# Rows normed where they are gathered, and a search shared by VectorE and ScalarE over two 15-bit numbers, in a macaron block with two expert layers

## The chip, the cores and the metric

The kernel runs on one core of a Trainium2 chip. Its five engines run side by side, each with its own queue: TensorE (PE; its weight loads are shown as PEld), VectorE (DVE), ScalarE (ACT), GpSimd (POOL) and SyncE (SP), which here only issues DMAs. The metric is the device time of one execution in microseconds, as the median of the runs shown. Everything is float32 unless a type is named.

## The reference

x has 4 x 2048 = 8192 rows of 256. A feed-forward layer of 8 experts, an attention layer, and the same feed-forward layer again are added to it:

```python
x = x + 0.5 * ffn(layernorm(x), router_w, wg, wu, wd)
x = x + attn(layernorm(x), ...)
x = x + 0.5 * ffn(layernorm(x), router_w, wg, wu, wd)
```

The feed-forward layer routes each row to two of eight experts, and each expert takes at most 1280 rows:

```python
probs = softmax(xf @ router_w.T)                  # 8192 x 8
topw, topi = top_k(probs, 2); topw = topw / (topw.sum(-1) + 1e-06)
order = lexsort((-fw, fe))                        # by expert, then by falling weight
rank = arange(2 * N) - starts[se]; keep = rank < 1280
g, u = disp @ wg, disp @ wu                       # an expert's kept rows, 256 -> 1024
eo = (silu(g) * u) @ wd                           # 1024 -> 256
out[st] += eo * sw * keep
```

The attention has 16 heads of 16. Its keys are a softmax over the rows of the softmaxed queries, so that keys and values meet in one 16 x 16 matrix per head and batch (`ctx`), which is applied to the queries.

## The kernel before

It has five stages in a row: first router and route, experts, attention, route, experts again.

*Router.* The 8192 rows lie in `xw`, 64 tiles of 128 rows, each row followed by 8 columns for the expert weights and 8 for 0/1 flags (`W` = 272). `choose` computes softmax, top two and weights; its last two operations (L272, L273), on GpSimd, put half the weight and the flag "is routed" behind the row. `norm_row` (L194 on GpSimd, L196 on ScalarE) norms a row tile in place by `rstd` and `shift`, and `write_rows` (L276) sends the tiles to `rows` in DRAM. In the first route `norm_beside` does this beside the search; in the attention stage `choose_on` advances `choose` in small steps between the attention's own work and norms two tiles at a time. The last 20 tiles are normed after the stage.

*Route.* For each expert the 1280 largest weights have to be found. The weights are transposed to 128 partitions of 512 (`wt`, L295), 16 partitions for each expert. The limit is found bit by bit over the 30 bits of the float's pattern: the candidate `cand` is compared with all weights on VectorE, which sums the hits (`above`, L309, with `accum_out=part`); a matmul with `group4` adds the 16 partitions of an expert and tells by its sign whether enough are above (`reach`, L308 and L310); VectorE picks the next candidate from `low` and `high` (L314 to L316). Each step waits for the one before. After each step `next(beside, None)` issues a piece of other work: in the first route the norms and the preparation of the attention weights. Then ties are settled (L322 to L338, two scans), the result `St` is transposed back on PE (`back`, L343) and split into `slot_hi` and `slot_lo`.

*Experts.* `RowList` turns the slots of one expert into a list of row numbers by matmuls with 0/1 matrices (`ix`, L413; for the first expert the matrices `lo` come from VectorE, L401). `gather` (L471) fetches five tiles of 128 rows by indirect DMA from GpSimd's queue; `blank` (L483, L485) multiplies a row by its flag, so that places that are not taken are zero; `turn` (L496, L499) transposes the tiles on PE. The products run over 16 chunks of 640 rows (two for each expert) in a Strassen-Winograd scheme with 7 instead of 8 block products; the sums of weight blocks that it needs are `ws` (`sums_of_w`, eight VectorE operations of 128x512) and `wds`. For the first expert `ws` is formed by VectorE between the list and the first chunk, and the first `wds` sum stands before the sixth product:

```python
            gather(1)
            for m in range(2):
                sums_of_w(0, m)
            blank(0, *range(TURN))
...
            sum_of_wd(k, 0)
            sixth_product(0)
            sum_of_wd(k, 1)
```

*Order.* In router, route, attention and experts the order of PE, VectorE and ScalarE is that of the program (`manual_schedule`); in the experts GpSimd is left to the scheduler. SP issues its DMAs as a queue.

Of the kernel before, what the change touches and what calls it, by code (L numbers as in the profile page):

```python
# [1 line left out]

# [6 lines left out]
F32 = mybir.dt.float32  # L9
F16 = mybir.dt.float16  # L10
# [8 lines left out]
P = 128  # L19
# [3 lines left out]
NOWHERE = 8191  # L23


@with_exitstack
def macaron_kernel(
# [33 lines left out]
    W = D + 2 * E  # L61
# [66 lines left out]
    group4 = const.tile([P, P], F16, name="group4")  # L128
    nc.gpsimd.tensor_scalar(group4, heads, 4.0, None, ALU.mult)
    short = const.tile([P, 1], F16, name="short")  # L130
    nc.gpsimd.memset(short, -(CAP - 1.0) / (P // E))
# [57 lines left out]

    def norm_row(xw, t, gpsimd=False):  # L190

        row, by, of = xw[:, t, 0:D], rstd[:, t : t + 1], shift[:, t : t + 1]
        if gpsimd:
            nc.gpsimd.tensor_scalar(row, row, by, of, ALU.mult, ALU.add)  # L194
        else:
            nc.scalar.activation(row, row, AF.Identity, bias=of, scale=by)  # L196

    def norm_beside(xw, to, steps=iter(())):


        t, busy = 0, True
        while t < T or busy:
            busy = next(steps, 0) != 0
            for gpsimd in (True, False) if busy else (False, True, False):
                if t < T:
                    norm_row(xw, t, gpsimd)
                    t += 1
                    if t % NJ == 0:
                        write_rows(xw, to, slice(t - NJ, t))
            yield  # L210

    def choose(xw, w, ts, pool):
# [60 lines left out]
        nc.gpsimd.tensor_scalar(xw[:, ts, D + E :], by_token, 0.0, None, ALU.is_gt)  # L273
# [4 lines left out]
    def route(w, pool, ppool, beside=iter(())):  # L278
# [5 lines left out]
        def new(name):  # L284
            return pool.tile(FULL, F32, name=name)
# [8 lines left out]
        wt = new("wt")  # L294
        nc.vector.tensor_copy(wt, ps.rearrange("p r q -> p (r q)"))  # L295
# [4 lines left out]
        cand, low, high = one("cand", I32), one("low", I32), one("high", I32)  # L300
        cand_f = cand.bitcast(F32)
        part = one("part", F16)
        above, tie = new("above"), new("tie")
        nc.vector.memset(cand, 1 << 29)
        for bit in range(29, -1, -1):

            reach = ppool.tile([P, 4], F32, tag="cnt", name="reach", bufs=2)
            nc.tensor.matmul(reach[:, :1], group4, short, start=True, stop=False)  # L308
            nc.vector.tensor_scalar(above, wt, cand_f, 0.0, ALU.is_ge, ALU.add, accum_out=part)  # L309
            nc.tensor.matmul(reach[:, :1], group4, part, start=False, stop=True)  # L310
            next(beside, None)

            half = 1 << (bit - 1) if bit else 0
            nc.vector.tensor_scalar(low, cand, (1 << bit) | half, None, ALU.bitwise_xor)  # L314
            nc.vector.tensor_scalar(high, cand, half, None, ALU.bitwise_xor)
            nc.vector.tensor_scalar(  # L316
                cand_f, reach[:, :1], low.bitcast(F32), high.bitcast(F32), ALU.max, ALU.min
            )
# [3 lines left out]
        nc.vector.tensor_scalar(tie, wt, cand_f, 0.0, ALU.is_equal, ALU.add, accum_out=parts[:, 1:2])  # L322
        nc.vector.tensor_scalar(above, wt, cand_f, 0.0, ALU.is_gt, ALU.add, accum_out=parts[:, 0:1])
# [16 lines left out]

        ps = ppool.tile([P, GT, P], F32, tag="turn", name="back", bufs=1)
# [110 lines left out]
    def experts(name, src, dst, wait_for, weights, wpool, pool, ppool):  # L452
# [8 lines left out]
        lists, got, xTs, turned, ws, wds, xs = {}, {}, {}, {}, {}, {}, {}  # L461
# [15 lines left out]
        def blank(k, *tiles):  # L477
            for i in tiles:
                if k < len(chunks):
                    e, r = chunks[k][0], got[k][i]  # L480
                    has = r[:, D + E + e : D + E + e + 1]
                    if k == 0 and i % 2:
                        nc.vector.tensor_scalar(r[:, 0:D], r[:, 0:D], has, None, ALU.mult)  # L483
                    else:
                        nc.scalar.mul(r[:, 0:D], r[:, 0:D], has)  # L485
# [21 lines left out]
        def sums_of_w(e, m):  # L507

            if e >= E:
                return  # L510
            if m == 0:
                ws[e] = pool.tile([P, 2, 4, FH], F32, tag="ws", name="ws", bufs=1)
            v, o = weights[e][m], ws[e]
            a11, a12, a21, a22 = v[:, 0, :FH], v[:, 1, :FH], v[:, 0, FH:], v[:, 1, FH:]
            tt(o[:, m, 0, :], a21, a22, ALU.add)
            tt(o[:, m, 1, :], o[:, m, 0, :], a11, ALU.subtract)
            tt(o[:, m, 2, :], a11, a21, ALU.subtract)
            tt(o[:, m, 3, :], a12, o[:, m, 1, :], ALU.subtract)
# [40 lines left out]
        def units(k):  # L559
# [75 lines left out]
            sum_of_wd(k, 0)  # L635
            sixth_product(0)
            sum_of_wd(k, 1)
# [92 lines left out]
        def early(k, p):  # L730
# [4 lines left out]
            elif p == 2:  # L735
                blank(k + 1, 0, 1, 2, 3)
            elif p == 3:
                blank(k + 1, 4)
# [97 lines left out]
        with tc.manual_schedule(engines=ENGINES - {mybir.EngineType.Pool}):  # L836
# [9 lines left out]
            for m in range(2):  # L846
                sums_of_w(0, m)
            blank(0, *range(TURN))
            for q in (0, 2):
                turn(0, q)  # L850
            blank(0, *range(TURN, CH))
# [72 lines left out]
    def attention(xw, w, to, weights, pool, ppool):  # L924
# [151 lines left out]
        choosing, chosen = [], []  # L1076
# [247 lines left out]
```

## Time and profile before

| what | us |
|---|---|
| median of 3 runs | 1992.24 (1991.15 to 1992.62) |
| the profiled execution | 1991.06, of which span 1989.1 |
| first router, to the first search step | about 0 to 50 |
| first search, list and gather, to the first full run of products | 50 to 126.6 |
| first experts | 126.6 to 893 |
| attention | 893 to 1137 |
| second search, list and gather | 1137 to 1213 |
| second experts | 1213 to 1989.1 |

Over the whole span PE is busy 92%, DVE 70%, ACT 48% and POOL 51%. The chain that ended last is 82% PE. Mean duration of one operation: `above` (L309) 0.746 us, `cand` (L316) 0.276, `low` and `high` 0.15 and 0.14, the read-out of the sum 0.085; `ws` and `wds` on VectorE 0.68 to 0.69; `norm_row` 0.59 on ScalarE and 0.56 on GpSimd; `blank` 0.50 on ScalarE. In the groups a line gives source line, engine, operation, output and input tile and count, and for one tile the least, median and greatest duration in ns and the first and last start; in a timeline the first two numbers are start and duration in us, and the bracket at the end tells how long the engine had been idle and whose work ended that.

### The profile page before, as it was taken

To read this page: it belongs to the slowest core of one execution; us is meant where nothing else is said; L and a number is where in the kernel's file an instruction comes from. 1 tells how busy PE (TensorE), PEld (TensorE's weight loads), DVE (VectorE), ACT (ScalarE), POOL (GpSimd) and SP (SyncE) were. 2 spreads that over 40 slices of the span, in tenths; PEclk is the share of its full clock that TensorE was granted. 3 is DMA by queue.
4 is the path that set the end of the run, shared out by engine and by line. 5 is a ranking of instruction groups with operands and counts; after the bars stand their busy time and mean duration, and the time that the engine had idled before them with its cause. 6 is when DMAs were issued, how large, how long until landed. Compare 5 with 4: busy or idle time off the path is not lost.

```text
span 1989.1 us, 25375 instructions
## 1 busy us (share of the span) xinstructions
PE 1831.6 (92%) x8756; PEld 1332.4 (67%) x8756; DVE 1401.2 (70%) x2555; ACT 957.6 (48%) x2371; POOL 1019.5 (51%) x1017
## 2 busy tenths in 40 slices
PE   6379999999999999999999627999999999999997
PEld 5247777777777777777887415777777777777776
DVE  7866767676767676647788886676767676676763
ACT  5435454554546463325565405554646363737332
POOL 4435555555555555535555304555555555555552
PEclk8589999999999999999999858999999999999999
DMA  9911313222222221125002531222222222231121
GB/s 357 309 29 28 91 31 88 58 61 71 49 70 49 71 49 28 28 24 172 33 33 88 191 135 29 67 52 71 49 70 49 70 49 75 44 94 29 31 29 19
DMA packets 99935, 147.66 MB, mean 74 GB/s; under 512 B 7512, under 2 KB 86368, under 8 KB 99680
## 3 DMA queue, kind: packets, MB, share of 16 engines
q1 hardware_dynamic: 69072, 102.77, 15.2%
q0 software_dynamic: 30720, 43.27, 13.4%
q8 instruction: 69, 1.13, 0.2%
q14 instruction: 58, 0.48, 0.1%
q10 hardware_dynamic: 16, 0.01, 0.0%
HBM read 98.84 MB, written 55.57 MB: 78 GB/s over the span
## 4 chain that ended last, share of the span: by engine, by line
PE 82%; DVE 8%; issue 1%; POOL 1%; ACT 1%; DMA 1%; POOLq 0%; DVEq 0%; ACTq 0%; SPq 0%
PE mm L570 48%; PE mm L770 23%; PE tr L496 2%; PE back L722 2%; PE qp L957 1%; PE pc L1012 1%; PE ix L413 1%; PE py L1070 1%; DVE above L309 1%; PE mm L828 1%; DVE st L1082 1%; DVE xw L1080 1%; DVE q L965 1%; DVE m L970 0%; DVE z L979 0%
## 5 line engine op out<-in xcount | busy, mean ns | idle before, releaser
L570 PE MATMUL mm<-xs,ws 128*128 128x320 f32 x1536 | 476.9, 433 | 3.9 <-DVE u L502 3.0
L505 POOL TENSOR_TENSOR ct<-ct 128x320 f32<-128x320 f32 x360 | 338.8, 941 | 190.2 <-DVE ct L601 166.7
L570 PEld LDWEIGHTS mm<-xs,ws 128*128 128x128 f32 x1536 | 284.3, 190 | 113.0 <-DVE u L502 4.1
L502 DVE TENSOR_TENSOR ct<-u,mm 128x640 f32<-128x640 f32 x256 | 209.8, 819 | 180.1 <-PE mm L570 169.0
L502 DVE TENSOR_TENSOR ct<-ct,mm 128x640 f32<-128x640 f32 x288 | 235.8, 819 | 74.6 <-PE mm L570 74.1
L598 ACT ACTIVATE ct<-ct 128x960 f32<-128x960 f32 (+2 forms) x192 | 141.7, 738 | 298.7 <-DVE ct L502 298.7
L471 POOL DMA_INDIRECT r<-rows,ixs x160 | 157.6, 985 | 235.9 <-ACT eo L703 172.8
L770 PE MATMUL mm<-ct,wds 128*128 128x320 f32 x960 | 278.5, 433 | 0.0
L407 ACT ACTIVATE lo<-from_below,behind_lo 128x129 f16<-128x129 f32 x896 | 272.9, 395 | 0.0
L770 PEld LDWEIGHTS mm<-ct,wds 128*128 128x128 f32 x960 | 178.5, 190 | 73.2 <-DVE ct L502 6.4
L770 PE MATMUL mm<-ct,wdt 128*128 128x320 f32 x720 | 213.5, 433 | 0.0
L704 POOL DMA_INDIRECT acc<-eo,ixs x80 | 127.7, 1596 | 141.9 <-ACT eo L703 124.0
L704 POOL DMA_INDIRECT out_dram<-eo,ixs x80 | 127.6, 1596 | 141.9 <-ACT eo L703 124.0
L570 PE MATMUL mm<-xsT,wgt 128*128 128x320 f32 x512 | 183.5, 440 | 0.0
L570 PE MATMUL mm<-xsT,wut 128*128 128x320 f32 x512 | 180.7, 435 | 0.0
L601 DVE TENSOR_TENSOR ct<-ct 128x640 f32<-128x640 f32 (+1 forms) x128 | 166.0, 1297 | 18.8 <-ACT ct L598 18.8
L502 DVE TENSOR_TENSOR u<-p,mm 128x640 f32<-128x640 f32 x128 | 105.0, 821 | 88.3 <-PE mm L570 80.6
L770 PEld LDWEIGHTS mm<-ct,wdt 128*128 128x128 f32 x720 | 132.1, 190 | 47.5
L607 ACT COPY p<-mm 128x640 f32<-128x640 f32 x128 | 88.3, 690 | 154.3 <-PE mm L570 154.3
L570 PE MATMUL mm<-xsT,ws 128*128 128x320 f32 x512 | 158.7, 432 | 0.0
L703 ACT ACTIVATE eo<-back,r 128x256 f32<-128x256 f32 x150 | 65.0, 478 | 152.7 <-PE back L722 152.7
L570 PEld LDWEIGHTS mm<-xsT,wut 128*128 128x128 f32 x512 | 97.7, 191 | 40.7 <-issue 0.8
(226 smaller groups left out, 2820.0 us busy)
## 6 DMA issues: line engine op xcount, KB each, us to landing
wgt<-in_L_ffn_wg_dram SPq DMA_DIRECT2D x16, 1024.0 KB, 5.0
wut<-in_L_ffn_wu_dram SPq DMA_DIRECT2D x16, 1024.0 KB, 7.5
wdt<-in_L_ffn_wd_dram SPq DMA_DIRECT2D x16, 1024.0 KB, 5.3
rows<-xw SPq DMA_DIRECT2D x7, 2176.0 KB, 15.0
xw<-in_L_attn_x_dram SPq DMA_DIRECT2D x16, 512.0 KB, 8.4
out_dram<-xw SPq DMA_DIRECT2D x16, 512.0 KB, 2.9
xw<-acc SPq DMA_DIRECT2D x15, 512.0 KB, 8.8
r<-rows,ixs POOLq DMA_INDIRECT x160, 2.8
```

Of the source, the lines that this page charges most:

```text
L407: nc.scalar.activation(lo[:, t, :], from_below, AF.Sign, bias=at, scale=1.0)
L471: nc.gpsimd.indirect_dma_start(out=r, out_offset=None, in_=src[:, :], in_offset=bass.IndirectOffsetOnAxis(ap=lists[e][:, i : i + 1], axis=0),)
L496: nc.tensor.transpose(ps[:, (i - i0) * P : (i - i0 + 1) * P], got[k][i][:, c * P : (c + 1) * P], ident)
L502: nc.vector.tensor_tensor(o, a, b, op)
L505: nc.gpsimd.tensor_tensor(o, a, b, op)
L570: nc.tensor.matmul(ps, a, b, start=start, stop=True, skip_group_check=not start)
L598: nc.scalar.activation(h(p)[:, qs, :], h(p)[:, qs, :], AF.Silu)
L601: engine.tensor_tensor(h(p)[:, qs, :], h(p)[:, qs, :], hT(p)[:, qs, :], ALU.mult)
L607: nc.scalar.copy(p1, ps)
L703: nc.scalar.mul(eo, ps, got[k][i][:, D + e : D + e + 1])
L704: ins = nc.gpsimd.indirect_dma_start(out=dst[:, :], out_offset=bass.IndirectOffsetOnAxis(ap=lists[e][:, i0 + i : i0 + i + 1], axis=0), in_ ...
L770: nc.tensor.matmul(ps, a(p), b(p), start=(p == 0 and not more), stop=(p == NF - 1), skip_group_check=more)
```

## The change

- Rows are written to DRAM as they are, not normed, and the norm moves to the gathered tiles: `choose` puts, behind each row and for each expert, flag x `rstd` and flag x `shift` (two more GpSimd operations, `W` = 280), and `norm` takes the place of `blank` with these two as scale and bias. `norm_row` and `norm_beside` are gone, and rows are written as soon as `choose` is done.
- The search goes over two numbers of 15 bits, kept as floats (`key`: the upper 15 bits for steps 0 to 14; then the difference to the number found, together with the lower 15 bits, for steps 15 to 29). In each step VectorE compares 304 of the 512 columns (`part`), and ScalarE takes Sign of the other 208 and sums it (`signs`). Two matmuls (`group_v`, `group_s`) add the two counts. `above` and `tie` become float16.
- The weight sums of the first expert are formed on GpSimd beside the search, by `weight_sums`, in both routes. In the first route they stand ahead of the attention weights' preparation.
- 14 matmuls without use (`stay_busy`) stand before the back transposes.
- In the first chunk the first `wds` sum stands behind the sixth product.
- SP's queue: in the second route the last two row writes now stand ahead of the expert weights' loads; before, two of these loads (`wgt`, `wut`) stood ahead of them.

```diff
+KEYS = 1 << 15
+SIGNS = 208
...
-    W = D + 2 * E
+    W = D + 3 * E
...
-    nc.gpsimd.tensor_scalar(group4, heads, 4.0, None, ALU.mult)
+    group_v = const.tile([P, P], F16, name="group_v")
+    nc.gpsimd.tensor_scalar(group_v, heads, float(KEYS), None, ALU.mult)
+    group_s = const.tile([P, P], F16, name="group_s")
+    nc.gpsimd.tensor_scalar(group_s, heads, -KEYS / 2.0, None, ALU.mult)
+
     short = const.tile([P, 1], F16, name="short")
-    nc.gpsimd.memset(short, -(CAP - 1.0) / (P // E))
+    nc.gpsimd.memset(short, SIGNS / 2.0 - (CAP - 1.0) / (P // E))
...
         nc.gpsimd.tensor_scalar(xw[:, ts, D : D + E], by_token, 0.5, None, ALU.mult)
-        nc.gpsimd.tensor_scalar(xw[:, ts, D + E :], by_token, 0.0, None, ALU.is_gt)
+        factor, by = (xw[:, ts, D + k * E : D + (k + 1) * E] for k in (1, 2))
+        nc.gpsimd.tensor_scalar(factor, by_token, 0.0, None, ALU.is_gt)
+        nc.gpsimd.tensor_tensor(by, factor, tok(shift[:, ts]), ALU.mult)
+        nc.gpsimd.tensor_tensor(factor, factor, tok(rstd[:, ts]), ALU.mult)
...
             nc.tensor.transpose(ps[:, r, :], by_group[:, r, :], ident)
-        wt = new("wt")
-        nc.vector.tensor_copy(wt, ps.rearrange("p r q -> p (r q)"))
-        cand, low, high = one("cand", I32), one("low", I32), one("high", I32)
-        cand_f = cand.bitcast(F32)
-        part = one("part", F16)
-        above, tie = new("above"), new("tie")
-        nc.vector.memset(cand, 1 << 29)
-        for bit in range(29, -1, -1):
+        bits = ps.rearrange("p r q -> p (r q)").bitcast(I32)
+        ints, key, upper, lower = new("ints", I32), new("key"), new("upper"), new("lower")
+        nc.vector.tensor_scalar(ints, bits, 15, None, ALU.logical_shift_right)
+        nc.vector.tensor_scalar(key, ints, 0.5, None, ALU.add)
+        nc.gpsimd.tensor_scalar(upper, key, float(KEYS), None, ALU.mult)
+        cand, low, high, base = one("cand"), one("low"), one("high"), one("base")
+        part, signs = one("part", F16), one("signs", F16)
+        above, tie, sign = new("above", F16), new("tie", F16), new("sign", F16)
+        CV = GT * P - SIGNS
+        nc.vector.memset(cand, KEYS / 2.0)
+        for step in range(30):
 
             reach = ppool.tile([P, 4], F32, tag="cnt", name="reach", bufs=2)
-            nc.tensor.matmul(reach[:, :1], group4, short, start=True, stop=False)
-            nc.vector.tensor_scalar(above, wt, cand_f, 0.0, ALU.is_ge, ALU.add, accum_out=part)
-            nc.tensor.matmul(reach[:, :1], group4, part, start=False, stop=True)
+            nc.tensor.matmul(reach[:, :1], group_v, short, start=True, stop=False)
+            with nc.allow_low_precision(reason="whole numbers up to SIGNS"):
+                nc.scalar.activation(
+                    sign[:, CV:], key[:, CV:], AF.Sign, bias=cand, scale=-1.0, accum_out=signs
+                )
+            nc.vector.tensor_scalar(above[:, :CV], key[:, :CV], cand, 0.0, ALU.is_ge, ALU.add, accum_out=part)
+            nc.tensor.matmul(reach[:, :1], group_s, signs, start=False, stop=False)
+            nc.tensor.matmul(reach[:, :1], group_v, part, start=False, stop=True)
             next(beside, None)
 
-            half = 1 << (bit - 1) if bit else 0
-            nc.vector.tensor_scalar(low, cand, (1 << bit) | half, None, ALU.bitwise_xor)
-            nc.vector.tensor_scalar(high, cand, half, None, ALU.bitwise_xor)
-            nc.vector.tensor_scalar(
-                cand_f, reach[:, :1], low.bitcast(F32), high.bitcast(F32), ALU.max, ALU.min
-            )
+            unit = float(KEYS >> step % 15 + 1)
+            half = unit / 2 if unit > 1 else 0.0
+            nc.vector.tensor_scalar(low, cand, half - unit, None, ALU.add)
+            nc.vector.tensor_scalar(high, cand, half, None, ALU.add)
+            if step == 0:
+                nc.vector.tensor_scalar(ints, bits, KEYS - 1, None, ALU.bitwise_and)
+                nc.gpsimd.tensor_scalar(lower, ints, 0.5, None, ALU.add)
+            nc.vector.tensor_scalar(cand, reach[:, :1], low, high, ALU.max, ALU.min)
+            if step == 14:
+                nc.vector.tensor_scalar(base, cand, float(KEYS), KEYS / 2.0, ALU.mult, ALU.add)
+                nc.vector.scalar_tensor_tensor(key, upper, base, lower, ALU.subtract, ALU.add)
+                nc.vector.memset(cand, KEYS / 2.0)
 
 
         parts = one("parts", F16, 2)
-        nc.vector.tensor_scalar(tie, wt, cand_f, 0.0, ALU.is_equal, ALU.add, accum_out=parts[:, 1:2])
-        nc.vector.tensor_scalar(above, wt, cand_f, 0.0, ALU.is_gt, ALU.add, accum_out=parts[:, 0:1])
+        nc.vector.tensor_scalar(cand, cand, 0.5, None, ALU.add)
+        nc.vector.tensor_scalar(tie, key, cand, 0.0, ALU.is_equal, ALU.add, accum_out=parts[:, 1:2])
...
 
+        stay_busy(ppool.tile([P, GT, P], F32, tag="turn", name="turn", bufs=1)[:, 0, :], 14, P)
         ps = ppool.tile([P, GT, P], F32, tag="turn", name="back", bufs=1)
...
-    def experts(name, src, dst, wait_for, weights, wpool, pool, ppool):
+    def weight_sums(engine, e, wpool, weights, ws, *which):
+
+        if e >= E:
+            return
+        for m in which:
+            if m == 0:
+                ws[e] = wpool.tile([P, 2, 4, FH], F32, tag="ws", name="ws", bufs=1)
+            v, o = weights[e][m], ws[e]
+            a11, a12, a21, a22 = v[:, 0, :FH], v[:, 1, :FH], v[:, 0, FH:], v[:, 1, FH:]
+            for to, a, b, op in (
+                (0, a21, a22, ALU.add), (1, o[:, m, 0, :], a11, ALU.subtract),
+                (2, a11, a21, ALU.subtract), (3, a12, o[:, m, 1, :], ALU.subtract),
+            ):
+                engine.tensor_tensor(o[:, m, to, :], a, b, op)
+                yield
...
-        def blank(k, *tiles):
+        def norm(k, *tiles):
             for i in tiles:
                 if k < len(chunks):
                     e, r = chunks[k][0], got[k][i]
-                    has = r[:, D + E + e : D + E + e + 1]
+                    row = r[:, 0:D]
+                    by, of = (r[:, D + j * E + e : D + j * E + e + 1] for j in (1, 2))
                     if k == 0 and i % 2:
-                        nc.vector.tensor_scalar(r[:, 0:D], r[:, 0:D], has, None, ALU.mult)
+                        nc.vector.tensor_scalar(row, row, by, of, ALU.mult, ALU.add)
                     else:
-                        nc.scalar.mul(r[:, 0:D], r[:, 0:D], has)
+                        nc.scalar.activation(row, row, AF.Identity, bias=of, scale=by)
 
         def turn(k, q):
...
             x4 = xs.pop(k)
-            sum_of_wd(k, 0)
+            if k > 0:
+                sum_of_wd(k, 0)
             sixth_product(0)
+            if k == 0:
+                sum_of_wd(k, 0)
             sum_of_wd(k, 1)
             if k > 0:
...
-            for m in range(2):
-                sums_of_w(0, m)
-            blank(0, *range(TURN))
+            norm(0, *range(TURN))
             for q in (0, 2):
                 turn(0, q)
-            blank(0, *range(TURN, CH))
+            norm(0, *range(TURN, CH))
...
                 first_router(xw, w, pool, ppool)
-                steps = norm_beside(xw, rows[0], steps)
+                for b in range(B):
+                    write_rows(xw, rows[0], slice(b * NJ, (b + 1) * NJ))
+                steps = chain(weight_sums(nc.gpsimd, 0, wpool, weights, ws, 0, 1), steps)
                 route(w, pool, ppool, steps)
...
-                route(w, pool, ppool)
+                route(w, pool, ppool, weight_sums(nc.gpsimd, 0, wpool, weights, ws, 0, 1))
```

## The prediction

> **What bounds it now.** I read the busy time by stage first, since the share of the whole span mixes two kinds of stage (columns: stage in us, its length, then busy us and instruction count of PE, PEld, DVE, ACT, POOL, the granted clock, DMA share, GB/s):
>
> ```profile
> core 0: us, PE busy (x) PEld busy (x) DVE busy (x) ACT busy (x) POOL busy (x), PEclk, DMA share, GB/s
> ...
> 48.60:92.00 43.40, 14.90 (x88) 11.04 (x89) 36.76 (x157) 19.97 (x43) 21.91 (x33) 0.50 1.05 336
> ...
> 126.60:893.00 766.40, 765.93 (x3455) 545.76 (x3455) 523.65 (x723) 382.96 (x978) 410.01 (x345) 1.00 0.24 52
> ...
> 1137.00:1179.00 42.00, 5.80 (x61) 3.99 (x60) 36.61 (x155) 5.59 (x12) 0.00 (x0) 0.50 0.62 217
> 1179.00:1186.00 7.00, 1.28 (x6) 0.82 (x5) 5.59 (x12) 0.00 (x0) 0.00 (x0) 0.50 0.00 0
> 1186.00:1196.00 10.00, 5.26 (x65) 3.06 (x65) 8.09 (x17) 0.27 (x1) 0.62 (x1) 0.60 0.01 3
> 1196.00:1213.00 17.00, 7.58 (x22) 4.13 (x22) 9.49 (x18) 6.06 (x16) 10.37 (x10) 0.70 0.29 82
> ```
>
> The experts (766 us, twice) are PE without a gap: what ACT pays there is covered. The search, the first list and the first gather stand before each of them with PE waiting, 76 to 78 us each time. All that this change can win lies there. One step of the search, from the timeline of the second route (start us, duration us):
>
> ```profile
> 1141.95 0.74 DVE L309 TENSOR_SCALAR_CACHE_REDUCE above<-wt,cand 128x512 f32<-128x512 f32 x1
> 1142.62 0.09 DVE L309 DVE_READ_ACCUMULATOR above<-wt,cand 128x1 f16 x1
> 1142.62 0.15 DVE L314 TENSOR_SCALAR low<-cand 128x1 int32<-128x1 int32 x1
> ...
> 1142.76 0.16 PE L310 MATMUL reach<-part,group 128*128 128x1 f16 x1 [1.13 <-DVE above L309]
> ...
> 1142.96 0.28 DVE L316 TENSOR_SCALAR cand<-reach,low,high 128x1 f32<-128x1 f32 x1
> 1143.27 0.75 DVE L309 TENSOR_SCALAR_CACHE_REDUCE above<-wt,cand 128x512 f32<-128x512 f32 x1
> ```
>
> A step is one closed chain: count, read-out, matmul, new candidate, 1.32 us from start to start; 30 of them. ACT's prices for what it is to take over come from the groups of lines L407 (129 columns, pointer bias), L989 (256, one pointer) and L196 (256, two):
>
> ```profile
> L407 ACT ACTIVATE lo<-from_below,behind_lo x896: 385/392/425, 123.0 to 1832.5; 128x129 f16<-128x129 f32 x180
> ...
> L989 ACT ACTIVATE xs<-xw,rstd x64: 492/498/519, 908.2 to 1097.4; 128x256 f32<-128x256 f32 x64
> ...
> L196 ACT ACTIVATE xw<-xw,shift,rstd x102: 583/588/603, 38.3 to 1142.0; 128x256 f32<-128x256 f32 x102
> ```
>
> And GpSimd's gathers behind the second route, while DVE forms the weight sums (until 1201.05) and after:
>
> ```profile
> 1196.98 1.33 POOL L471 DMA_INDIRECT r<-rows,ixs  x1 [9.57 <-DVE ws L502]
> 1198.61 1.34 POOL L471 DMA_INDIRECT r<-rows,ixs  x1 [0.30 <-issue]
> 1200.26 1.01 POOL L471 DMA_INDIRECT r<-rows,ixs  x1 [0.30 <-issue]
> 1201.57 0.95 POOL L471 DMA_INDIRECT r<-rows,ixs  x1 [0.30 <-issue]
> ```
>
> **The search step.** DVE keeps 304 of 512 columns. Its tensor_tensor takes 0.692 us for 512 columns and 0.488 for 320, 1.06 ns a column, so 208 columns less are 0.22 us: were DVE alone in the chain, a step would be 1.325 - 0.22 = 1.105 us, and the matmul of `part` would start 0.81 - 0.22 = 0.59 after the count. ACT runs beside it. From 129 to 256 columns L407 and L989 differ by 0.106 us, 0.84 ns a column, so Sign on 208 costs 0.392 + 79 x 0.84 = 0.46. Its accumulator must be read out: the trace has no such operation on ACT. From below, DVE's own read-out is 0.085 and starts 0.07 before the listed end of the count; from above, ACT's smallest operations (128x8, 128x16) take 0.18, here laid wholly behind Sign. With 0.03 for the start and 0.05 to PE the matmul of `signs` starts at 0.53 to 0.72, and `part` follows behind one more weight load, 0.02 (as the load and matmul of L308 follow each other) to 0.10. Not before 0.59, then, and not after 0.82: a step of 1.105 to 1.335. I take the 0.18 read-out overlapped by 0.09, as successive L196 overlap (18 in 8.94 us), and a cheap weight load: 0.03 + 0.46 + 0.09 + 0.05 + 0.02 = 0.65, step 1.17. 30 x (1.325 - 1.17) = 4.65 us less per route (range 6.6 less to 0.3 more).
>
> **What the two 15-bit numbers add, per route, all on DVE in the chain.** At the start `ints` from PSUM takes the place of the copy `wt` (0.69); `key` is new, SBUF to SBUF: between L349 (512 int16, 0.29) and the copy (0.69), taken as 0.45, since L483 does 256 f32 in 0.35. In step 0 the second `ints` is 0.69, of which 0.2 falls into DVE's wait for `reach`: 0.5. After step 14 `base` 0.15, `key` 0.75 (as L338) and the memset 0.06: 0.96. `cand` + 0.5: 0.15. Sum +2.06. `above` + `tie` in f16 gets cheaper: L382 does 1024 f16 in 0.684, so 512 in about 0.41 against 0.69: -0.28.
>
> **The moved weight sums.** The eight sums (4.9 us of DVE) leave the place behind the list and go to GpSimd inside the search, 8 x 1.06 (L972, same shape) = 8.5 us there, on an engine that the second search shows with 0.00 busy. Queued behind them on GpSimd are the attention weights' preparation and `behind_lo` (first needed by the second list): covered. Only `lower` stands behind the first sum, and that sum waits for wgt. In the second route SP now issues the last two row writes (2.7 MB) ahead of wgt, which before went out at 1135.96. At the 350 to 400 GB/s of that stretch, rows and wgt (3.8 MB) need some 11 us from 1137, landing near 1149; sum and `lower` (1.1 each) end near 1152; DVE asks for `lower` at 1138.4 + 0.5 + 15 x 1.17 = 1156. Cover of 4 us; beyond it each us costs one.
>
> What follows DVE's release: the gathers. The two beside the weight sums took 1.33 and 1.34 against 0.95, and the first started 1.0 after `ixs` was written (1.1 in the first route). The third gather, whose tile releases the first turn, should go out earlier by 0.3 to 0.8 of lag plus 0.39 + 0.39 (first route 0.42 + 0.24): taken as 1.2 (0 to 1.9). The page SBUF — State Buffer, "Who interferes with whom", says that a tensor_tensor on DVE does not stall descriptor generation, as an inference; by it this term is zero and the total 2.4 us smaller. The gathers' own durations speak otherwise, and I go by them.
>
> **Order of the first chunk.** `u` comes before the first `wds` sum: the sum (0.60 in the chain ahead of `u`) leaves the path, and the next idle of DVE (0.84) covers it: -0.6. The norm instead of the blank: L196's 0.59 against L485's 0.50, one tile on the path: +0.1; the other 150 are beside PE.
>
> **The 14 matmuls before the back transposes.** They start when L326 is done and take 14 x 0.23 (four cold transposes span 1.10, the last 0.42 long) = 3.2 us; `St` is ready 4.9 after, 4.6 with the cheaper sum, so they delay nothing. Warm, four transposes take 0.44 (L722 in the experts) against 1.10, and the list's matmuls end some 0.3 earlier behind the last `lo`. Clock 0.60 in 1186 to 1196 means that it rose about 2 us before the end, some 4 us into the list's matmuls. Taken as -0.8 (0 to -1.0). The page TensorE: Matmul & The Clock Gate, Part 1, wants about 3.4 us of sustained work; by it 3.2 us fall short, the term is zero, and the total 1.6 us smaller.
>
> **First route only.** GpSimd holds L272 and L273, 1.95 each, when the search starts at 49.8, and now two more of about 2.0. DVE operations beside GpSimd work do stretch (line L226's `b`, 0.17 to 0.21 alone, took 1.03 beside L982), so `key` may wait up to one such operation: +1.2 (0 to 2.2). ACT's preparations (means, woT, bob: 0.18 to 0.58) stand between Signs, with 0.5 free in each step: +0.3. Rows are written from about 57 instead of 61 to 86: covered until the gather at 109.
>
> **Attention.** 48 L196 leave ACT's loop, but a pair of tiles takes 6.17 us with and without them, and DVE is busy 19.28 of 20 us at 1020 to 1040: nothing. Each `choose` has two more GpSimd operations of 0.4 to 0.7 ahead of the next norm or softmax products: +0.8 in all (0 to 1.5).
>
> **Sum.** Second route: -4.65 + 2.06 - 0.28 - 1.2 - 0.6 + 0.1 - 0.8 = -5.37. First: the same + 1.5 = -3.87. Attention +0.8. Total -8.4 us. The profiled execution took 1991.06 (span 1989.1 and 1.96 around it), 1.18 under the median 1992.24; the sum is a difference, so from the median: 1983.8, given as 1984.
>
> **Rivals.** *DVE alone sets the step* (1.105): ACT's read-out hides. 60 x 0.065 = 3.9 us more won: 1980. For it: 0.53 is possible for `signs`. Chance 0.25.
> *ACT sets the step, slower than before.* ACT's fixed cost is high (0.28 of L407's 0.39 is not columns) and a read-out that pays it again behind Sign gives 0.03 + 0.46 + 0.28 + 0.05 + 0.10 = 0.92 for `part`, or 1.435 a step: 60 x 0.265 = 15.9 more than forecast, 2000. All other terms together are +0.9, so it decides against the change from a step of 1.31. Against it: small ACT operations overlap their predecessor. Chance 0.07.
> *The chip's side terms eat it*: no gain at the gathers (2.4), none of the clock (1.6), `key` held 2.2 (1.0), 0.7 more in attention: 1989.5. Chance 0.13.
> *The change does not reach the chain*, because `lower` waits for wgt: landing past 1155 stalls step 14; 5 us late gives 1989. Chance 0.05.
> The forecast keeps 0.50.
>
> **Numbers.** Runs of this kernel differ by 0.1%, so 0.2%, 4 us, is what can be told from no change. Faster: forecast and first rival, and the few cases in which only one of the side terms fails, 0.78; same: the side terms' rival and the late `lower`, 0.15; slower 0.07. From 1978.5 (first rival with the clock and gather terms at their good ends) to 1992 (a step of 1.30 with the other terms as taken).
>
> **What would show it.** Steps of 1.17 with `part`'s matmul 0.65 after the count; ACT's read-out under 0.2; gathers of 0.95 from the first, the third some 1.2 us earlier behind `ixs`; back transposes in about 0.5; attention's pairs still 6.17 apart; the experts' 766 us unchanged. Steps above 1.31, a stall of DVE at step 14, or longer experts would prove it wrong.

## The result and the profile after

The changed kernel took 1991.3 us (median of 14 runs, 1988.61 to 1993.8), the kernel before 1991.78 on the same chips (14 runs, 1989.15 to 1992.76): a ratio of 1.0001 with a 95% interval of 0.9994 to 1.0008. No change that can be told, where 8 us less were forecast. The profiled execution took 1989.32 (span 1987.5), 1.74 less than the one before the change.

The same stages of the changed kernel, busy time by stage:

```profile
48.20:90.20 42.00, 15.62 (x118) 12.08 (x119) 32.28 (x161) 18.86 (x67) 23.30 (x19) 0.50 1.01 324
125.80:893.50 767.70, 767.14 (x3456) 545.59 (x3456) 521.88 (x724) 389.92 (x978) 410.40 (x345) 1.00 0.24 52
1136.40:1177.80 41.40, 6.57 (x89) 4.75 (x89) 32.86 (x161) 16.91 (x60) 13.37 (x11) 0.50 0.63 221
1177.80:1185.00 7.20, 6.25 (x34) 5.82 (x33) 5.40 (x12) 0.00 (x0) 0.00 (x0) 0.66 0.00 0
1185.00:1194.60 9.60, 5.25 (x65) 3.06 (x65) 7.86 (x16) 0.27 (x1) 1.12 (x1) 0.64 0.01 3
```

Two things are to be seen. The search still fills about 41 us, with DVE now idle for 8.5 of them in the second route. And the first experts, PE without a gap in both kernels, are 767.7 us long instead of 766.5.

One step of the search, from the timeline:

```profile
1160.48 0.47 ACT L301 ACTIVATE sign<-key,cand 128x208 f16<-128x208 f32 x1 [0.66 <-DVE cand L316]
1160.48 0.53 DVE L304 TENSOR_SCALAR_CACHE_REDUCE above<-key,cand 128x304 f16<-128x304 f32 x1
1160.86 0.19 ACT L301 ACTIVATION_READ_ACCUMULATOR sign<-key,cand 128x1 f16 x1
1160.94 0.09 DVE L304 DVE_READ_ACCUMULATOR above<-key,cand 128x1 f16 x1
1161.10 0.16 PE L305 MATMUL reach<-signs,group_s 128*128 128x1 f16 x1 [1.00 <-ACT sign L301]
1161.39 0.28 DVE L316 TENSOR_SCALAR cand<-reach,low,high 128x1 f32<-128x1 f32 x1 [0.24 <-PE reach L299]
1161.70 0.47 ACT L301 ACTIVATE sign<-key,cand 128x208 f16<-128x208 f32 x1 [0.66 <-DVE cand L316]
```

A step is 1.22, not 1.17. ACT's read-out ends 0.57 after the start (DVE's ends 0.55), the matmul of `signs` starts at 0.62 and names ACT as the one that ended its wait. `cand` then waits 0.24 for `reach`.

Three places around the search that the sum had otherwise, from the timeline (first route, second, first):

```profile
100.84 0.69 DVE L379 TENSOR_TENSOR hi<-counts,slot_hi 128x1024 f16<-128x1024 int16 x1 [3.22 <-DMA rows<-xw]
...
1156.47 1.46 DVE L320 SCALAR_TENSOR_TENSOR key<-upper,base,lower 128x512 f32<-128x512 f32 x1
...
90.88 4.76 PE L166 MATMUL turn<-row_of_ones,ident 128*128 128x128 f32 x28
```

`hi`, the first operation of the list, waits 3.22 us for the row writes, though it reads nothing of theirs: its tile lies in memory that the router's `xw` held. Before the change the same operation waited for no DMA:

```profile
99.75 1.05 DVE L374 TENSOR_TENSOR hi<-counts,slot_hi 128x1024 f16<-128x1024 int16 x1 [0.19 <-issue]
```

`key` at step 14 costs 1.46 us in the second route and 1.22 in the first, instead of 0.75. The 14 matmul calls are 28 instructions, an f32 matmul being two, and take 4.76 us in the first route and 5.54 in the second.

Where the time went, stage by stage, in us (after less before; the forecast's own term beside it):

| stage | forecast | measured |
|---|---|---|
| first route, to the first product behind `u` (126.59, 125.79) | -3.87 | -0.80 |
| first experts (766.51, 767.68) | 0 | +1.17 |
| attention, to the second route's `ints` (244.04, 242.89) | +0.8 | -1.15 |
| second route (75.96, 74.22) | -5.37 | -1.74 |
| second experts, to the last scatter (766.61, 767.88) | 0 | +1.27 |
| end of the span and outside it | 0 | -0.49 |
| sum | -8.4 | -1.74 |

Of the attention's -1.15 a part is likely chance: in the profile before, the clock stood at 0.50 from 1108.7 to 1112.1, in the one after it did not fall (more on this at the end). The rest of it was not tested.

### The profile page after: what moved, and what is told of

Its sections match the earlier page's. It is cut to its first block, busy times and chain, and to the rows that moved or that the text cites. A ratio compares the mean times of both kernels' runs of the same rounds, so it can differ in the third digit from the quotient of the medians.

```text
span 1987.5 us, 25620 instructions
## 1 busy us (share of the span) xinstructions
PE 1842.7 (93%) x8872; PEld 1341.5 (67%) x8872; DVE 1378.9 (69%) x2551; ACT 955.9 (48%) x2389; POOL 1038.9 (52%) x1024
## 3 DMA queue, kind: packets, MB, share of 16 engines
q8 instruction: 70, 1.15, 0.3%
## 5 line engine op out<-in xcount | busy, mean ns | idle before, releaser
L614 DVE TENSOR_TENSOR ct<-ct 128x640 f32<-128x640 f32 (+1 forms) x128 | 160.7, 1256 | 21.6 <-ACT ct L611 21.6
```

Of the source, the lines that this page charges most:

```text
L614: engine.tensor_tensor(h(p)[:, qs, :], h(p)[:, qs, :], hT(p)[:, qs, :], ALU.mult)
```

## The experiments

Each is the changed kernel with one edit, up to those under "All together". "Changed" is the changed kernel. Five of them were executed once and are read by their traces, not by their times: `SIGNS = 176` (1989.24 us) and no matmuls (1989.44), beside 1991.36 before on that chip; VectorE alone (2000.04) and GpSimd at step 14 (1994.18), beside 1994.77; the sums back on VectorE (1993.72), beside 1995.87.

**The longer experts.** Theory: the norm, longer than the blank, stands ahead of a copy that PE waits for. Rival: the wider rows, or the weight sums' new pool.

```
             elif p == 2:
-                norm(k + 1, 0, 1, 2, 3)
+                norm(k + 1, 0, 1, 2)
             elif p == 3:
-                norm(k + 1, 4)
+                norm(k + 1, 3, 4)
```

> One edit to the changed kernel: of the five norms of a chunk's gathered tiles, the fourth goes from the third place in ScalarE's program (p == 2, ahead of eight `lo` operations and the copy of PSUM `p1`) to the next place (p == 3). In the changed kernel each pair of experts' chunks takes 0.20 us more than before at six boundaries of either stage, where `p1` starts 0.20 later and the first product behind it waits. Theory: the norm (0.60 us against the blank's 0.51) makes four of them 0.36 longer, and that is more than the slack ahead of `p1`. Then the first experts end 1.17 us earlier relative to their first product (766.5 us instead of 767.7), the second 1.27 earlier, and the kernel is about 2.4 us faster than the changed kernel: 1989 median. Rival: the longer experts come from the wider rows (1120 bytes instead of 1088) or from the weight sums' new pool; then they stay at 767.7 and 767.9.

Measured 1988.75 us (11 runs) against 1991.36 before on that chip: ratio 0.9986, interval 0.9977 to 0.9995. From the first down product to the first of the last but one chunk either stage of the experts is 673.68 us long, against 674.9 in the changed kernel and 673.9 before. The theory holds; wider rows and the pool, unchanged here, cost nothing that is seen. ACT's timeline ahead of one of those copies: the kernel before, the changed kernel, and this one, in which the same place comes 2.1 us earlier in the span:

```profile
432.10 1.71 ACT L485 ACTIVATE r<-r 128x256 f32<-128x256 f32 x4
433.71 2.45 ACT L407 ACTIVATE lo<-from_below,behind_lo 128x129 f16<-128x129 f32 x8
436.05 0.68 ACT L607 COPY p<-mm 128x640 f32<-128x640 f32 x1
```

```profile
431.93 2.07 ACT L507 ACTIVATE r<-r 128x256 f32<-128x256 f32 x4
433.90 2.44 ACT L412 ACTIVATE lo<-from_below,behind_lo 128x129 f16<-128x129 f32 x8
436.24 0.68 ACT L620 COPY p<-mm 128x640 f32<-128x640 f32 x1
```

```profile
430.26 1.59 ACT L507 ACTIVATE r<-r 128x256 f32<-128x256 f32 x3
431.74 2.45 ACT L412 ACTIVATE lo<-from_below,behind_lo 128x129 f16<-128x129 f32 x8
434.09 0.68 ACT L620 COPY p<-mm 128x640 f32<-128x640 f32 x1
```

Four norms are 0.36 longer than four blanks (2.07, 1.71), the eight `lo` follow without a gap, and the copy `p` starts 0.36 later against what PE does beside it, of which PE sees 0.20. This happens where a chunk also makes a list's `lo`: six times in either stage.

**The wait of `hi`.** Theory: the row writes end late because the second expert's weights go out ahead of them.

```
-                    write_rows(xw, rows[0], slice(b * NJ, (b + 1) * NJ))
+                    written = write_rows(xw, rows[0], slice(b * NJ, (b + 1) * NJ))
...
-        load_expert(1, wpool, weights)
+        load_expert(1, wpool, weights, [written])
```

The three loads then wait for the last row write (the lines that do this are left out here).

> One edit to the changed kernel: the loads of the second expert's weights (3 x 1 MB) go out on SyncE behind the first route's row writes, instead of ahead of them. Theory: `hi` (L379), whose tile takes over the router's `xw`, waits 3.2 us for the row writes, which end at 98.7 behind a saturated DMA; 3.1 MB at 345 GB/s are 9 us, so the rows end near 90, `hi` starts 0.1 to 0.3 behind `slot_lo` at 97.6 to 97.9, and the first product and all after it come 2.9 to 3.2 us earlier. Rival 1: something else releases `hi` (the rest of the router's pool), it still starts at 100.8, nothing is gained. Rival 2: `hi` starts at 97.7, but the weights' transfer now lies beside the first gathers at 107 and stretches their 2.7 us landing, so 1 us or less is left.

Measured 1987.57 us (11 runs) against 1991.36: ratio 0.9985, interval 0.9976 to 0.9994. From the timeline:

```profile
90.65 6.29 PE L166 MATMUL turn<-row_of_ones,ident 128*128 128x128 f32 x28
...
99.05 1.11 DVE L379 TENSOR_TENSOR hi<-counts,slot_hi 128x1024 f16<-128x1024 int16 x1
```

The wait for the rows is gone: the last row write lands at 91.36 (in the changed kernel at 100.72, not at 98.7 as the expectation has it), and the weights, which wait for it, are issued at 91.4. But in this execution only 1.36 us were gained at the first down product (152.10 against 153.46), not 3. The clock stayed at 0.50 until past 96, the 28 matmul instructions took 6.29 us, and the back transposes, whose input was ready at 95.3, started at 97.0. And `hi` itself took 1.11 us instead of 0.69, since it now ran beside GpSimd's `behind_lo` (99.00 to 99.62). The place was taken by the next wait, and that one is also the change's. The profiled execution is the slowest of the eleven (1991.67 us); the median lies 4.1 us under it, and no trace shows how much of the 3 us the faster ones gained here. Neither rival is seen: no late release, and the gathers take what they took.

**ScalarE's share.** `SIGNS = 176` for 208:

> One number of the changed kernel: ScalarE's Sign takes 176 columns instead of 208, VectorE 336 instead of 304. Theory (ScalarE's read-out sets the step): Sign is 32 x 0.84 ns = 0.027 us shorter, VectorE's count 0.034 longer; the step falls from 1.222 to 1.195 to 1.21, less where VectorE's leg comes level. Rival (VectorE already sets it): the step grows by 0.034 to 1.256.

The step is 1.20 (1160.47 to 1161.67). Sign fell to 0.44, VectorE's count rose to 0.56, and the two matmuls now start 0.04 apart: the legs are level. ACT's read-out did set the step at 208, by 0.02 us, no more.

**VectorE alone.** `SIGNS = 0`, without the Sign and its matmul:

> The changed kernel without ScalarE's share (SIGNS = 0): VectorE counts all 512 columns of the 15-bit keys, ScalarE's Sign and the matmul of `signs` are left out. Theory: VectorE's leg goes back to what it was, a step of 1.31 to 1.33 instead of 1.222, so that the sharing is worth 0.09 to 0.11 a step, 2.7 to 3.3 us in each search, and the search with the two 15-bit numbers alone is longer than before by the overhead of the two numbers (2.0 to 2.6 us a route). Rival: ScalarE's second reader of `key` slowed VectorE's count down; then the step without it is under 1.29.

```profile
1161.55 0.75 DVE L300 TENSOR_SCALAR_CACHE_REDUCE above<-key,cand 128x512 f16<-128x512 f32 x1
...
1162.87 0.74 DVE L300 TENSOR_SCALAR_CACHE_REDUCE above<-key,cand 128x512 f16<-128x512 f32 x1
```

Again 1.32 a step. From the first `reach` to the last one the searches take 42.16 and 42.44 us, against 39.42 and 39.72 in the changed kernel and 40.56 and 40.44 before. So the sharing is worth 2.7 us a search, and the two numbers' overhead (1.6 and 2.0 here, 0.5 of either ahead of the first count) takes most of it back.

**The 14 matmuls.** Left out:

> One edit to the changed kernel: the 14 matmuls (28 instructions, 4.76 and 5.42 us) ahead of the back transposes are left out. Theory: the transposes start when `St` is ready (0.2 us earlier in the first route, 0.9 in the second) and take 1.10 instead of 0.67, VectorE's `slot` and `hi` follow as before the change (`hi` 1.05 instead of 0.69), and the list's matmuls end at the same distance: from `St` to the end of `ix` within 0.5 us of the changed kernel in the second route, so the 14 matmuls bring at most 0.5 us where 1.6 were forecast for both routes. Rival: without them the clock stays low through the list and the second list ends 0.8 or more later behind `St`, as forecast.

In the second route, from the last `reach` to the end of `ix`: 17.07 us, against 17.47 with them. They cost 0.4 there. The transposes take 1.08 instead of 0.66, but start when `St` is ready; `hi` takes 0.69 either way and the list's matmuls 4.91 either way, being bound by DVE's `lo`. In the first route the wait for the rows hid the difference.

**GpSimd at step 14.** In the second route the sums, in the first the attention's preparations on GpSimd, are put behind step 14 in the order in which the program is written:

> One edit to the changed kernel: GpSimd's weight sums begin behind step 14 in the second route, and the attention's preparations on GpSimd behind step 14 in the first, so that GpSimd is idle while VectorE forms `key` from `upper`, `base` and `lower`. Theory: `key` (L320) falls from 1.22 and 1.46 to about 0.75, so 0.5 and 0.7 us come back, and `lower` (1.50 beside VectorE) is unchanged; the eight sums still end before the first gather. Rival: the 1.2 to 1.5 are the price of this operation's two f32 tensors, whatever GpSimd does; then it stays.

In the first route `key` fell from 1.22 to 0.75. In the second it stayed at 1.27, because the edit did not move the sums: they wait for `wgt` alone, which landed at 1151, and GpSimd runs ahead of the search whatever its place in the text. Only `lower` went ahead of them (1142.20 instead of 1149.65). The theory holds by the first route and by the next run, and the rival falls: `key` takes 0.75 in both where GpSimd is idle.

The traces say what sets the price. Where `key` starts while GpSimd is in a tensor_tensor, it ends 0.55 us after that operation does. In the changed kernel:

```profile
1156.13 1.26 POOL L470 TENSOR_TENSOR ws<-ws,wut 128x512 f32<-128x512 f32 x1
1156.47 1.46 DVE L320 SCALAR_TENSOR_TENSOR key<-upper,base,lower 128x512 f32<-128x512 f32 x1
1157.34 1.72 POOL L470 TENSOR_TENSOR ws<-wut 128x512 f32<-128x512 f32 x1
```

GpSimd's operation ends at 1157.39 and `key` at 1157.93; the next on GpSimd is the longer for it. In the first route it is 70.17 and 70.73, in this run's second route 1160.23 and 1160.78. So `key` pays for what is left of GpSimd's operation, and how much that is differs from run to run.

**The sums back on VectorE**, behind the first list:

> The changed kernel with its weight sums put back where they were: eight sums on VectorE behind the first list instead of on GpSimd inside the search; the rest of the change stays. By the prediction's term (the sums beside the gathers cost 1.2 us up to the third gather): first and second gather take 1.33 again, the lag from `ixs` to the first gather grows, and the third gather starts 4.8 us behind `ixs`. By the changed kernel's trace (lag 0.9 in the second route without the sums, 1.0 with them; gathers of 1.13 and 0.97 against 1.33 and 1.34): 4.3 us instead of 3.6, so the move is worth 0.7 a route. Beside it, with GpSimd idle in the second search, `key` at step 14 takes 0.75 instead of 1.46, which gives the 0.7 back there.

```profile
1196.25 0.17 DVE L438 CAST ixs<-ixf 128x16 int32<-128x16 f32 x1
1197.41 1.33 POOL L492 DMA_INDIRECT r<-rows,ixs  x1 [8.78 <-DVE ws L470]
1199.05 1.34 POOL L492 DMA_INDIRECT r<-rows,ixs  x1 [0.30 <-issue]
1200.69 1.00 POOL L492 DMA_INDIRECT r<-rows,ixs  x1 [0.30 <-issue]
```

The same place of the changed kernel:

```profile
1194.44 0.17 DVE L438 CAST ixs<-ixf 128x16 int32<-128x16 f32 x1
1195.51 1.13 POOL L492 DMA_INDIRECT r<-rows,ixs  x1 [8.69 <-DVE ixs L438]
1196.94 0.97 POOL L492 DMA_INDIRECT r<-rows,ixs  x1 [0.30 <-issue]
1198.22 0.95 POOL L492 DMA_INDIRECT r<-rows,ixs  x1 [0.30 <-issue]
```

From the start of the cast to the third gather 4.44 us in both routes with the sums beside it, 3.78 (second route) and 4.08 (first) without: the move is worth 0.66 and 0.36, not 1.2. The lag between `ixs` and the first gather is some 1.0 in either. `key` takes 0.75 in both routes. So the move gives at the gathers 0.4 to 0.7 and pays 0.5 to 0.7 of it at step 14.

**All together.** Five edits: the norm, the rows, `SIGNS = 184`, no matmuls, the order at step 14.

> The changed kernel with five edits: the fourth norm one place later, the second expert's weights behind the row writes, ScalarE 184 columns instead of 208, no matmuls ahead of the back transposes, GpSimd idle at step 14. If the terms add up: experts 2.4 us, `hi` 3.1, steps 60 x 0.02 = 1.2, the 14 matmuls 0.4 in the second route and 0.2 to 1.7 in the first, `key` 1.2: 8.3 to 9.8 us under the changed kernel, median about 1982.5, which would beat both kernels. Rival: the first route's gains run into the next wait there (the DMA, the transposes at a low clock), and only the experts, the steps and `key` are left: 4.8 us, 1986.5.

Measured 1987.75 us (5 runs) against 1994.77 before on that chip: ratio 0.9962, interval 0.9948 to 0.9975, about 7.5 us less. In the profile the first route ends `ix` 17.27 us behind the last `reach` (19.64 changed), the step is 1.20, and the experts are 1.0 to 1.1 shorter than those of the runs with the norms unmoved on that chip (675.87 and 675.63, against 676.8). By the ratios (0.9962, and 1.0001 for the changed kernel) that is 7.8 us under the changed kernel, between the two expectations and nearer to the first. One term of it is luck: in the second route the edit did not move the sums, and `key` took 0.75 because it started 0.15 us before GpSimd's operation ended.

The same with 8 matmul calls:

> The same five edits, but with 8 matmuls (16 instructions) ahead of the back transposes instead of none. Theory: 16 x 0.17 to 0.225 = 2.7 to 3.6 us are over before `St` is ready at 4.6, so they delay nothing, and PE then idles 1 to 2 us; if the clock holds over that gap, the transposes take 0.67 instead of 1.10 and this version is 0.4 us a route faster than the one without; if it does not hold, the two are equal. Rival: as with 14, they cost time.

Measured 1987.47 us (5 runs): ratio 0.9957, interval 0.9944 to 0.9971, about 8.5 us less than before. The two versions can't be told apart by the time. (In this profile `key` in the second route took 1.69, having started just behind a new operation of GpSimd.) In the second route the matmuls bring what was forecast for them: 16 instructions in 3.76 us, over before `St`, and the transposes at full clock, `ix` ending 16.61 behind the last `reach` instead of 17.06:

```profile
1176.73 3.76 PE L166 MATMUL turn<-row_of_ones,ident 128*128 128x128 f32 x16
...
1181.51 0.63 PE L348 MATMUL back<-ident,St 128*128 128x128 f32 x4 [1.01 <-DVE St L342]
```

In the first route the clock did not rise, the transposes took 1.08, and nothing was gained. Both versions are faster than the kernel before and, by their ratios to it, than the changed kernel.

**The clock in the attention.** A sixth edit, 4 matmul calls ahead of each sequence's `trg`:

> The five edits with 8 matmuls, and a sixth: 4 matmuls (8 instructions, 0.9 us) in the attention, into the wait of 1.45 us ahead of each sequence's `trg` transposes. In some profiles of these kernels, not in others, the granted clock falls to 0.5 to 0.8 for some 3.5 us just behind that wait (948 to 956, 1054 to 1062 us), and the stage is 1.5 us longer for each such fall. Theory: PE's idle time of 1.45 and 0.67 us there lets the clock fall by chance; with the wait filled it holds in all four sequences, no window between 900 and 1110 us shows a clock under 0.95, and the median is 1 to 3 us under that of the version without it against the same kernel before: a ratio near 0.995. Rival: the falls have another cause, or the matmuls delay `trg` by more than they bring; then the ratio stays at 0.9957 or rises, and falls are still seen.

Measured 1987.88 us (6 runs) against 1995.87: ratio 0.9966, interval 0.9954 to 0.9978. No gain. The filler did not fill the gap either: its tile was held by DVE, and PE idled 1.34 us ahead of it. This profile shows no fall of the clock between 900 and 1110 us, but neither did that of the changed kernel, so the test decides nothing; what the traces together show of the falls stands in the last section.

## Where the prediction held and where it failed, step by step

The time lies inside the stated range, at its upper end, but in the class that was given 0.15: the gain of 8 us did not come, and the forecast was 6.7 us off in the profiled pair. That the range held is in part luck: its upper end stood for a step of 1.30 with the other terms as taken, while the step is 1.22 and other terms failed. The rival that came nearest (the side terms) named two of the causes. The mechanism was right: the closed chain of the step got shorter, the two numbers' overhead was paid, the order of the first chunk gave its 0.6, `lower` had its cover (asked for at 1156.47, ready at 1151.15). The sizes and two covers failed.

*"a cheap weight load: 0.03 + 0.46 + 0.09 + 0.05 + 0.02 = 0.65, step 1.17"*: Sign is 0.47 and the read-out 0.19, 0.09 of it behind Sign as taken; but `part`'s matmul starts at 0.64. What failed is the term behind it: `cand` starts 0.27 after that matmul, not 0.20 as before the change, so the step is 1.22. 30 x 0.05 = 1.5 us a route. With VectorE alone, and so without the matmul of `signs` 0.02 ahead of `part`'s, it is 0.20 again (1163.68 to 1163.88): the second matmul is not free behind the first.

*"= 3.2 us; `St` is ready 4.9 after, 4.6 with the cheaper sum, so they delay nothing"*: priced at 14 instructions, they are 28. The price of 0.23 was that of one transpose, which is one instruction, while a call of these is two. The warm price, 0.44, counted four starts 0.11 apart; from the first start to the last end it is 0.60 by the same rows, and 0.66 was measured. -0.8 became +0.4 in the second route. And `ix`, which was to end 0.3 earlier, is bound by DVE. From the start of these matmuls the granted clock rose after 2.9 and 4.6 us in the changed kernel, 6.1 with the rows first, and not within the 3.76 us of the first route with 8 calls. The Trainium skill, page TensorE: Matmul & The Clock Gate, Part 1, has the clock rise after some 3.4 us of sustained work. With the prediction's 3.2 us this term was zero, nearer to what came than the forecast; with the 4.8 to 5.5 us that the matmuls took the clock should rise, as it did, though the rows spread more widely than one figure (the last section has why).

*"`key` 0.75 (as L338)"*: 1.22 and 1.46. The prediction itself put the sums on GpSimd at that time, and named "DVE operations beside GpSimd work do stretch" for the start of the search. There it charged 1.2 us that did not come (`key` at the start took 0.46); at step 14 it charged nothing, where `key` had to wait for GpSimd's running operation.

*"taken as 1.2"* for the gathers: 0.36 and 0.66. The lag from `ixs` to the first gather was counted on, and it is there without the sums too. The Trainium skill's page SBUF — State Buffer, "Who interferes with whom", by which a tensor_tensor does not stall descriptor generation, fits the lag; the gathers' own 1.33 against 0.97 to 1.13 do not fit it. The value lay between rule and forecast.

*"Rows are written from about 57 instead of 61 to 86: covered until the gather at 109"*: the wrong next user. The gather reads the rows, but the memory they are written from is needed by `hi` at 97.6. The writes began 6.6 us earlier (54.72 against 61.30) and ended later, since SyncE's queue holds them behind four copies of `acc` and the second expert's weights, and the DMA moved 340 to 356 GB/s from 70 us on in both kernels. The last of them landed at 100.72, against 98.92 before. What the first search won ahead of 100.8 was lost in this wait: 0.80 of the 3.87 us were left.

*"the other 150 are beside PE"* for the norm, and *"the experts' 766 us unchanged"*: +2.4 us. ACT is busy for half of that stage, which says nothing on the six places where norms, `lo` and a copy that PE needs stand in a row with no slack. The prediction named longer experts as a proof of error, but gave no price.

On the other side, in the second route the list's `lo` came 0.27 sooner behind `slot_lo` (`hi` 0.69 instead of 1.05, `hv` 0.73 instead of 0.49): in the second route of every profile with the change `hi` starts 0.05 ahead of `behind_lo` on GpSimd, before the change 0.10 behind it. The attention came out 1.95 better than forecast, part of it likely by the clock. The second route's 3.63 us of shortfall close to 0.1: 1.5 (steps) + 1.2 (matmuls) + 0.54 (gathers) + 0.71 (`key`) - 0.27 = 3.7.

The experiments give back what the list says: with the norm, the rows, the matmuls and the share put right, the kernel is 7 to 8.5 us under the kernel before, near the gain that was forecast for the change as it stood. What each of the edits brings to that time was not taken apart.

## What to carry to other kernels

Where an engine that is half idle gets a longer operation, look at the places where its queue runs without a gap up to something the busy engine waits for; the mean says nothing. Where a write to memory starts earlier, ask who needs its source next, not only who reads what it writes, and what stands ahead of it in the queue. Filler work has to end before the work that it prepares for: count its instructions, not its calls, at the slow clock's price.

## What the runs showed of the hardware

- ACT's read-out of an accumulator is an instruction of its own, 0.188 us, of which 0.09 lie behind the listed end of the ACTIVATE (second route of the changed kernel).
- VectorE's scalar_tensor_tensor over three f32 tensors in SBUF takes 0.75 us alone. Started while GpSimd was in a tensor_tensor, it ended 0.55 behind that one and took 0.95 to 1.69, in 14 places of these runs; where that operation had only 0.15 left, it took 0.75. In the second route GpSimd's next tensor_tensor then took 1.71 to 1.76, against 1.26 in the rest of the search.
- A later place in the program did not delay the sums on GpSimd: written behind step 14, they started at 1151.39, when `wgt` had landed, and step 14 ended at 1159.5.
- In all twelve traces the granted clock changes only at the edges of windows of 3.41 us, and where these lie against the program differs from run to run. In the two routes every rise (64) came behind a window in which PE was idle for 0.81 us or less, and every window at half clock with less than 0.60 of idle was followed by one. So filler matmuls raise the clock at the end of the first window that they all but fill, 2.8 to 6.2 us from their start in the 14 places with 28 instructions. The changed kernel's first route, where the first window did (the clock rose at 93.80), and that of the kernel with the rows first, where it took the second (96.78; stage columns as above):

```profile
90.39:93.80 3.41, 2.98 (x16) 2.97 (x16) 3.31 (x10) 0.00 (x0) 0.00 (x0) 0.50 1.12 344
```

```profile
89.96:93.37 3.41, 2.77 (x15) 2.77 (x15) 3.31 (x10) 0.00 (x0) 0.00 (x0) 0.50 0.31 51
93.37:96.78 3.41, 3.41 (x17) 3.31 (x16) 1.87 (x2) 0.00 (x0) 0.00 (x0) 0.50 1.01 414
```

- In the attention the granted clock falls in some executions to 0.50 for one such window: seven times in twelve traces, six of them at the turn of a sequence, where PE idles 1.45 to 1.77 us ahead of `trg` and 0.67 behind it. All seven came behind a window in which PE was idle for 1.71 to 2.13 us; of the 750 windows from 895 to 1112 us without a fall behind them, 745 had less than 1.7 of idle and none more than 1.77. So the same idle times let the clock fall or not, by whether one window holds enough of them. The kernel with the rows first (columns as above):

```profile
946.00:950.00 4.00, 1.87 (x15) 1.40 (x14) 3.77 (x11) 3.74 (x9) 2.49 (x3) 1.00 0.00 0
950.00:954.00 4.00, 4.00 (x15) 3.39 (x14) 0.61 (x2) 1.27 (x3) 0.96 (x3) 0.57 0.02 4
```

The eight `pc` matmuls there took 3.25 us, against 1.90 at full clock. That such falls, few or many, make the spread of 3 to 5 us between the runs of one kernel is likely (the runs' mean clocks go with their times), but no run here shows it.
